# Sixteen softmax blocks per group: which engine sums which block

## The chip, the cores and the metric

The kernel runs on one core of one Trainium2 chip. The metric is the device time of one execution in microseconds (us); of several runs the median is taken. The core has five engines that run side by side, each through its own instructions in order: TensorE (PE) multiplies matrices, VectorE (DVE), ScalarE (ACT) and GpSimd (POOL) work on elements, and SyncE (SP) issues DMA transfers. GpSimd can issue transfers too[...].

## The reference

The input is `x` with 8 samples of 2048 nodes and 256 channels, and an adjacency matrix `adj` of 2048 x 2048. One layer of masked attention with 8 heads of 32 channels, a feed-forward part, and three layer normalizations:

```python
qkv = jnp.einsum('fnc,ck->fnk', x, w_qkv)
q, k, v = jnp.split(qkv, 3, axis=-1)          # each reshaped to (F, N, H, D)
scores = jnp.einsum('fnhd,fmhd->fhnm', q, k) / jnp.sqrt(D)
scores = jnp.where(adj > 0, scores, -1e9)
attn = jax.nn.softmax(scores, axis=-1)
t = jnp.einsum('fhnm,fmhd->fnhd', attn, v).reshape(F, N, C)
x1 = _layernorm(x + t, ln1_g, ln1_b)
h = jax.nn.relu(x1 @ w1 + b1)
x2 = _layernorm(x1 + h @ w2 + b2, ln2_g, ln2_b)
return layernorm(x + x2)
```

The softmax needs, for every query and head, the sum of the exponentials over all 2048 keys. This sum, the denominator, is what the change is about.

## The kernel before

**Tiling.** The queries of a sample are cut into 4 chunks of 512 (`qc`), the heads into 2 halves of 4 (`g`), the keys into 16 blocks of 128 (`mb`). An item is `(f, qc, g, mb)`; there are 1024 of them, and they are worked off in this order by one loop written out in Python, `for t, (f, qc, g, mb) in enumerate(items)`. The 16 items of one `(f, qc, g)` are called a group here; there are 64 groups.

**One item.** Two steps ahead, `scores` (L230, L233) lets TensorE multiply keys by queries for 4 heads, and VectorE adds the mask while it copies the result into an SBUF tile `p` of 128 keys x 4 heads x 512 queries (1 MiB). One step ahead, `exponentials` (L237) takes the exponential of this tile on ScalarE. In its own step, `values` (L249) multiplies the tile by the values of its keys and gathers the result over the 16 blocks in PSUM. `add_up` (L264) follows.

**The denominator.** The column sums of a group's 16 tiles are wanted. TensorE could take all 16 by a product with a matrix of ones (L315), which costs 4 matrix products each. To spare TensorE, most tiles are first added together by others:

- `POOLED`: GpSimd adds tiles into the first of them by its own additions (L271).
- `MOVED`: two chains. A DMA issued by GpSimd (L268) adds a tile to the first tile of its chain while it moves it. Each DMA of a chain has to wait until the one before it has landed, since both add into the same tile. GpSimd waits with the issue in its queue.
- `ALONE`: one tile that goes to TensorE as it is.

So four tiles are left per group, and TensorE takes the column sums of these four (`denominator`, L297), one after the other into one PSUM bank: first the one that is alone, then the first chain, the second chain, and the sum of GpSimd. The chosen blocks are before the change

```python
    POOLED = (0, 3, 6, 8, 11, 13, 15)
    MOVED = ((1, 4, 7, 10), (2, 5, 9, 12))
    ALONE = 14
```

**The order of the work around it.** The products of `scores` and `values` leave some time in each step. It is given to side jobs, which are Python generators in the list `fill`, ordered by due time: projections of the next sample, transposes, denominators, and the tails (normalization, feed-forward, output) of finished chunks. `advance(t)` resumes them at the start of a step, before `scores`, `values` and `add_up` of that step. A job that yields `MORE` goes on when there is credit, mostly one step later; one that yields `WAIT` holds its place until a given step. The denominator of a group is started two steps after the group's last block; `late` says before which step a term must not be issued (`ready` is the last block's step plus 4). In the last group, where nothing follows, blocks from 11 on (`ENDED`) go to TensorE each by itself, in an order of its own.

**What else runs on GpSimd.** In the tails it makes the small operations of a norm (`rs`, `nb`, L283 to L287), on which ScalarE waits to scale the rows (L290); four passes over a tile `y` (L459, L461, L363, L365; some 2.7 us each); and issues two loads that add `x` to `y` (L339, L367). They stand in its queue where the step that issues them puts them, ahead of that step's `add_up`.

**Tiles.** The `p` tiles come from a pool of 12. A tile is free again after its sum, its DMA or its column sum.

Of the kernel before, what the change touches and what calls it, by code (L numbers as in the profile page):

```python
# [61 lines left out]
def fast_path(ctx, tc, cst, x, adj, out, RS):  # L62
# [29 lines left out]
    def transposes(ps, src, ident=ident):  # L92
        state["credit"] -= TURN
        for j, s in enumerate(src):
            nc.tensor.transpose(ps[:, j * P:(j + 1) * P], s, ident)  # L95
# [6 lines left out]
    def bank(dt=F32):  # L102
        shape = [P, CH] if dt == F32 else [P, 2, CH]
        if state["side"] is not None:
            i = 1 - state["side"]
            return ps_x[i].tile(shape, dt, name=f"x{i}")
        i = state["turn"]
        state["turn"] = (i + 1) % 5
        pool = ps_s[i] if i < 3 else ps_x[i - 3]
        return pool.tile(shape, dt, name=f"s{i}" if i < 3 else f"x{i - 3}")  # L110
# [143 lines left out]

    POOLED = (0, 3, 6, 8, 11, 13, 15)
    MOVED = ((1, 4, 7, 10), (2, 5, 9, 12))
    ALONE = 14

    ENDED = MB - 5
    SUM = 4
# [1 line left out]
    def add_up(item):  # L264
        f, qc, g, mb = item
        for chain in MOVED:
            if mb in chain[1:] and not ((f, qc, g) == items[-1][:3] and mb >= ENDED):
                nc.gpsimd.dma_start(PT[f, qc, g, chain[0]], PT.pop(item), accum_op=ALU.add)  # L268
        if mb in POOLED[1:] and not ((f, qc, g) == items[-1][:3] and mb >= ENDED):
            first = PT[f, qc, g, POOLED[0]]  # L270
            nc.gpsimd.tensor_tensor(first, first, PT.pop(item), ALU.add)  # L271
# [24 lines left out]

    def denominator(f, qc, g, ready):  # L297
        grp = (f, qc, g)
        blocks = [ALONE] + [chain[0] for chain in MOVED + (POOLED,)]
        late = {len(blocks) - 1: ready}  # L300
        if (f, qc, g) == items[-1][:3]:
            blocks = [POOLED[0], 11, 12, MOVED[1][0], 13, 14, MOVED[0][0], 15]
            late = {n: len(items) - k for n, k in ((2, 2), (3, 1), (4, 1), (5, 0), (6, 0), (7, 0))}
        yield BANK
        ps = bank()
        for n, block in enumerate(blocks):
            if n:
                yield MORE
            while state["now"] < late.get(n, 0):
                yield WAIT  # L310
            term = PT.pop((f, qc, g, block))
            state["credit"] -= 4 * CH
            for h in range(4):
                r = D * h
                nc.tensor.matmul(ps[r:r + D, :], cst["ones"], term[:, h, :], start=(n == 0), stop=(n == len(blocks) - 1))  # L315
        dT = op.tile([P, CH], F32, name="dT")
        nc.scalar.copy(dT, ps)
        yield 1
        yield BANK
        ps = bank()  # L320
        transposes(ps, [dT[:, j::TPC] for j in range(TPC)])
        if g == 0:
            RC[f, qc] = op.tile([P, TPC, H], F32, name="rc")
        rc = RC[f, qc]
        den = ps.rearrange("p (j c) -> p j c", c=P)[:, :, ::D]
        nc.vector.reciprocal(rc[:, :, 4 * g:4 * g + 4], den)
        nc.vector.tensor_tensor(RS[:, 0], RS[:, 0], den, ALU.add)
        nc.vector.tensor_tensor(RS[:, 1], RS[:, 1], den, ALU.min)
        if g == 1:
            begin = items.index((f, qc, g, LAST)) + SUM + 2  # L330
            start(begin, outcome(f, qc) if (f, qc) != (F - 1, NCK - 1) else finish(f, qc), begin)

    def outcome(f, qc):
        yield ROOM
        state["tails"] += 1
        xin = x[f, qc * CH:(qc + 1) * CH, :].rearrange("(p j) c -> p j c", p=P)
        y = yp.tile([P, TPC, C], F32, name="y")
        yield from divide(f, qc, y)
        nc.gpsimd.dma_start(y, xin, accum_op=ALU.add)  # L339
        begin = items.index((f, qc, 1, LAST)) + SUM + 2  # L340
        if (f, qc) == (F - 1, NCK - 2):
            start(begin + 5, tail(f, qc, y, xin, 2), begin + 8)
        else:
            start(begin + 10, tail(f, qc, y, xin), begin + 26)
# [92 lines left out]
    def finish(f, qc):  # L437
        y = yp.tile([P, TPC, C], F32, name="y")
        xr, xb = state["rows"]
        yield from divide(f, qc, y)  # L440
        yT, hT = (work.tile([P, 2, CH], F32, name=n) for n in ("turned", "hT"))
        dst = out[f, qc * CH:(qc + 1) * CH, :].rearrange("(p j) c -> p j c", p=P)
        both = [half_rows(h, y, xr, xb, yT, hT, dst) for h in range(2)]
        while both:
            for e in list(both):
                if next(e, both) is both:
                    both.remove(e)
# [40 lines left out]
    def start(t, gen, due):  # L488
        fill.append([t, gen, 1, due])
        fill.sort(key=lambda e: e[3])  # L490
# [108 lines left out]
    for t, (f, qc, g, mb) in enumerate(items):  # L599
# [26 lines left out]
        if mb == LAST and t + 1 < len(items):  # L626
            start(t + 2, denominator(f, qc, g, t + SUM), t + SUM + 4)
        if t == len(items) - 3:
            start(t, denominator(f, qc, g, t), t)
# [130 lines left out]
def kernel(  # L760
# [56 lines left out]
    nc.gpsimd.memset(RS[:, 1], 1.0)  # L817

    fast_path(tc, cst, x, adj, out, RS)


# [49 lines left out]
```

## Time and profile before

| what | value |
|---|---|
| time, median of 3 runs | 3245.36 us (3242.5 to 3246.28) |
| profiled execution | 3246.02 us |
| its span, first to last instruction | 3244.1 us |
| granted TensorE clock, mean | 0.985 |
| GpSimd sums (L271) | 381, mean 4793 ns, 1825.5 us busy |
| DMAs that add (L268) | 383 of 1 MiB, median 10.4 us from issue to landing |
| masked copies on VectorE (L233) | 2048, mean 1218 ns |
| exponentials on ScalarE (L237) | 1024, mean 1910 ns |
| waits of GpSimd's queue for landed DMAs, as such (L268) | 75.5 us in 32 |
| waits of ScalarE for GpSimd's `nb` (L290) | 40.4 us in 16 |

A row of the costliest groups reads: line, engine, operation, tile written and tiles read, their shapes, the number of instructions; then the busy time in us and the mean of one in ns; then the idle time of the engine just before these instructions and what ended most of it. "PE" are the matrix products, "PEld" the loads of their stationary operand, which overlap them. In a timeline the columns are the start in us, the duration in us, then engine, line, operation and tiles, and in brackets the idle time before and its releaser. A wait for several things is put down to the one that the profile saw last.

### The profile page before, as it was taken

The numbers are of one execution on the slowest core, as the hardware profiler recorded it, in microseconds if no ns is written. First come the engines' busy times: TensorE is split into PE (matmuls) and PEld (weight loads), VectorE is DVE, ScalarE is ACT, GpSimd is POOL, SyncE is SP. The second block draws the span as 40 slices with busy tenths as digits, with TensorE's granted clock in tenths as the row PEclk, the third lists the DMA queues.
The fourth block names the chain that finished last, engine by engine and source line by source line (L and its number), as shares of the span: only waits on it lengthen the run. The fifth ranks groups of instructions, "written<-read, shape, count | busy, mean of one in ns | idle before, by whom it ended". The sixth has DMA issues, their size and how long they took to land.

```text
span 3244.1 us, 68406 instructions
## 1 busy us (share of the span) xinstructions
PE 3109.4 (96%) x28996; PEld 979.0 (30%) x28996; DVE 2735.7 (84%) x3203; ACT 2435.8 (75%) x1941; POOL 2592.2 (80%) x1358
## 2 busy tenths in 40 slices
PE   7899999999999999999999999999999999998985
PEld 4222333223332233322233323323233323332222
DVE  4888888888888888888988888888888888888975
ACT  3667778777777777778777778777778777777774
POOL 0568888888878888788887888888888788878884
PEclk8899999999999999999999999999999999999998
DMA  9688779778879788788787879878788878877763
GB/s 320 145 181 185 183 176 199 178 177 196 181 176 207 171 188 193 159 195 200 178 181 174 185 174 221 177 167 198 173 192 197 177 168 198 181 171 161 166 145 86
DMA packets 153240, 590.52 MB, mean 182 GB/s; under 512 B 15040, under 2 KB 67776, under 8 KB 103904
## 3 DMA queue, kind: packets, MB, share of 16 engines
q0 software_dynamic: 64416, 434.80, 66.9%
q1 hardware_dynamic: 87696, 149.98, 13.1%
q8 instruction: 229, 3.75, 0.4%
q10 hardware_dynamic: 816, 1.31, 0.1%
q14 instruction: 83, 0.68, 0.1%
HBM read 146.67 MB, written 37.75 MB: 57 GB/s over the span
## 4 chain that ended last, share of the span: by engine, by line
PE 75%; DVE 7%; POOL 5%; issue 4%; DMA 4%; ACT 2%; DVEq 0%; POOLq 0%; ACTq 0%
PE s L230 27%; PE x L249 24%; PE x L54 14%; PE x L315 6%; DVE p L233 6%; PE x L95 4%; DMA p<-p 3%; POOL p L271 2%; ACT p L237 1%; DMA mask<-md 1%; POOL y L365 1%; DVE st L278 1%; POOL y L363 0%; POOL y L461 0%; POOL y L459 0%
## 5 line engine op out<-in xcount | busy, mean ns | idle before, releaser
L233 DVE TENSOR_TENSOR p<-s,mask 128x1024 f32<-128x1024 f32 x2048 | 2409.3, 1218 | 372.7 <-PE s L230 209.9
L237 ACT ACTIVATE p<-p 128x2048 f32<-128x2048 f32 x1024 | 1956.1, 1910 | 521.4 <-DVE p L233 465.6
L271 POOL TENSOR_TENSOR p<-p 128x2048 f32<-128x2048 f32 x381 | 1825.5, 4793 | 223.7 <-ACT p L237 221.3
L230 PE MATMUL s<-qT,kT 32*128 32x512 f32 x8192 | 1173.8, 643 | 40.8 <-DVE p L233 35.9
L249 PE MATMUL x<-p,v 128*32 128x512 f32 x8192 | 1096.0, 607 | 16.7 <-ACT p L237 16.4
L268 POOL DMA_DIRECT2D p<-p x383 | 359.3, 956 | 306.9 <-ACT p L237 88.3
L230 PEld LDWEIGHTS s<-qT,kT 32*128 32x128 f32 x8192 | 321.1, 183 | 644.7 <-DVE p L233 587.2
L249 PEld LDWEIGHTS x<-p,v 128*32 128x32 f32 x8192 | 161.6, 108 | 797.8 <-issue 310.6
L315 PE MATMUL x<-p,ones 128*32 128x512 f32 x2080 | 268.2, 594 | 17.9 <-POOL p L271 11.1
L290 ACT ACTIVATE y<-y,nb,rs 128x256 f32<-128x256 f32 x372 | 218.7, 590 | 40.4 <-POOL nb L287 40.4
L54 PE MATMUL x<-in,wqkv 128*32 128x512 f32 x1888 | 243.5, 592 | 0.0
L278 DVE BATCH_NORM_STATS2 st<-y 128x6 f32<-128x256 f32 x372 | 154.9, 416 | 5.1 <-DMA y<-in_x_dram 5.1
L54 PE MATMUL x<-turned,w1s 128*32 128x512 f32 x992 | 123.5, 596 | 0.4 <-ACT in L166 0.4
L54 PE MATMUL x<-w2s,hT 128*32 128x256 f32 x2016 | 121.8, 382 | 2.1 <-DVE y L483 2.1
L54 PEld LDWEIGHTS x<-wqkv,in 128*32 128x32 f32 x3584 | 102.2, 110 | 63.4 <-issue 58.9
L315 PEld LDWEIGHTS x<-p,ones 128*32 128x32 f32 x2080 | 66.3, 110 | 178.2 <-issue 140.4
L54 PE MATMUL x<-wqkv,in 128*32 128x128 f32 x3584 | 117.3, 273 | 0.0
L54 PEld LDWEIGHTS x<-in,wqkv 128*32 128x32 f32 x1888 | 61.7, 110 | 140.9 <-issue 113.7
L284 POOL TENSOR_TENSOR rs<-rs,mhalf 128x4 f32<-128x4 f32 x93 | 96.3, 1036 | 7.8
L54 PEld LDWEIGHTS x<-w2s,hT 128*32 128x32 f32 x2016 | 65.4, 111 | 75.0 <-issue 33.0
L363 POOL TENSOR_TENSOR y<-y,g2r 128x1024 f32<-128x1024 f32 x31 | 82.5, 2663 | 5.3 <-ACT y L290 5.3
L461 POOL TENSOR_TENSOR y<-y,be1b2r 128x1024 f32<-128x1024 f32 x31 | 83.0, 2679 | 0.6
(116 smaller groups left out, 1335.7 us busy)
## 6 DMA issues: line engine op xcount, KB each, us to landing
p<-p POOLq DMA_DIRECT2D x383, 1024.0 KB, 10.4
in<-xd SPq DMA_DIRECT2D x87, 512.0 KB, 10.6
mask<-md SPq DMA_DIRECT2D x248, 128.0 KB, 7.9
y<-in_x_dram POOLq DMA_DIRECT2D x62, 512.0 KB, 8.1
p<-in_adj_dram SPq DMA_DIRECT2D x16, 1024.0 KB, 10.7
out_dram<-y SPq DMA_DIRECT2D x31, 512.0 KB, 6.2
in<-in_x_dram SPq DMA_DIRECT2D x29, 512.0 KB, 15.5
xd<-in SPq DMA_DIRECT2D x28, 512.0 KB, 11.2
```

Of the source, the lines that this page charges most:

```text
L54: nc.tensor.matmul(out[r:r + D], lhsT[:, r:r + D], rhs, start=start, stop=stop)
L95: nc.tensor.transpose(ps[:, j * P:(j + 1) * P], s, ident)
L230: nc.tensor.matmul(ps2[half][:, j, :], KT[f, mb // TPC, g][r:r + D, (mb % TPC) * P:(mb % TPC + 1) * P], QT[f, qc, g][r:r + D, :], start=Tr ...
L233: nc.vector.tensor_tensor(pt[:, 2 * half:2 * half + 2, :], ps, MK[f, qc, mb // 2][:, mb % 2, None, :].to_broadcast([P, 2, CH]), ALU.add)
L237: nc.scalar.activation(PT[item], PT[item], AF.Exp, scale=1.0 / math.sqrt(D))
L249: nc.tensor.matmul(O[grp][r:r + D, :], V[f, mb // TPC, g][:, mb % TPC, r:r + D], PT[item][:, h, :], start=(mb == 0), stop=(mb == LAST))
L268: nc.gpsimd.dma_start(PT[f, qc, g, chain[0]], PT.pop(item), accum_op=ALU.add)
L271: nc.gpsimd.tensor_tensor(first, first, PT.pop(item), ALU.add)
L278: nc.vector.bn_stats(st, t[:, j, :])
L284: nc.gpsimd.tensor_tensor(rs, rs, cst["mhalf"], ALU.pow)
L290: nc.scalar.activation(t[:, j, :], t[:, j, :], AF.Identity, bias=nb[:, j:j + 1], scale=rs[:, j:j + 1])
L315: nc.tensor.matmul(ps[r:r + D, :], cst["ones"], term[:, h, :], start=(n == 0), stop=(n == len(blocks) - 1))
```

## The change

Blocks 10 to 15 change hands. The DMAs take blocks 11 and 13 in place of 10 and 12; GpSimd sums 10, 12 and 14 in place of 11, 13 and 15; block 15 in place of 14 goes to TensorE as it is. TensorE reads the four tiles of a group in another order: the one alone, the first chain, GpSimd's sum, the second chain, with the sum not before `ready - 1` and the second chain not before `ready`. In the last group, where blocks from 11 on are taken singly, the two chains change places.

```diff
-    POOLED = (0, 3, 6, 8, 11, 13, 15)
-    MOVED = ((1, 4, 7, 10), (2, 5, 9, 12))
-    ALONE = 14
+    POOLED = (0, 3, 6, 8, 10, 12, 14)
+    MOVED = ((1, 4, 7, 11), (2, 5, 9, 13))
+    ALONE = 15
...
     def denominator(f, qc, g, ready):
         grp = (f, qc, g)
-        blocks = [ALONE] + [chain[0] for chain in MOVED + (POOLED,)]
-        late = {len(blocks) - 1: ready}
+        blocks = [ALONE, MOVED[0][0], POOLED[0], MOVED[1][0]]
+        late = {2: ready - 1, 3: ready}
         if (f, qc, g) == items[-1][:3]:
-            blocks = [POOLED[0], 11, 12, MOVED[1][0], 13, 14, MOVED[0][0], 15]
+            blocks = [POOLED[0], 11, 12, MOVED[0][0], 13, 14, MOVED[1][0], 15]
```

## The prediction

> **What bounds the kernel now.** I read the page first, then the waits of TensorE, then the timeline of GpSimd, TensorE and ScalarE around the waits. "Group" means the 16 blocks of one (f, qc, g); there are 64, numbered from 0. "12D" is the DMA that adds block 12 to its chain, "13P" the GpSimd sum of block 13, a "step" one block on TensorE, and the four "terms" are the four column sums of a group (L315).
>
> ```profile
> PE 3109.4 (96%) x28996; PEld 979.0 (30%) x28996; DVE 2735.7 (84%) x3203; ACT 2435.8 (75%) x1941; POOL 2592.2 (80%) x1358
> ...
> L315 PE MATMUL x<-p,ones 128*32 128x512 f32 x2080 | 268.2, 594 | 17.9 <-POOL p L271 11.1
> ```
>
> TensorE is the bound: 96% of the span, and a step with a full side job starts 2.93 us after the one before, almost without spread. So only its stalls can be won. The list of what it waited for (us, times, longest):
>
> ```profile
> PE x L249 <- ACT p L237: 16.4, 10, 5.1
> ...
> PE x L315 <- POOL p L271: 11.1, 6, 2.1
> ...
> PE x L315 <- DMA p<-p: 6.9, 5, 3.9
> ```
>
> I took the same from the start times: a term normally starts 0.88 us after the block before it, and a block's values 1.07 us after its scores. What exceeds these between 100 and 3190 us is 21.0 us ahead of terms and 21.3 us ahead of values. Both repeat once per sample (eight groups, some 388 us).
>
> **Stall A, ahead of the terms**, in group 36. GpSimd: start, us, what, idle before.
>
> ```profile
> 1861.44 1.52 POOL L268 DMA_DIRECT2D p<-p  x1
> 1863.75 0.86 POOL L268 DMA_DIRECT2D p<-p  x1 [0.80 <-ACT y L290]
> 1864.33 4.90 POOL L271 TENSOR_TENSOR p<-p 128x2048 f32<-128x2048 f32 x1
> 1875.53 0.88 POOL L268 DMA_DIRECT2D p<-p  x1 [6.30 <-ACT v L215]
> 1876.13 2.67 POOL L363 TENSOR_TENSOR y<-y,g2r 128x1024 f32<-128x1024 f32 x1
> 1878.45 4.89 POOL L271 TENSOR_TENSOR p<-p 128x2048 f32<-128x2048 f32 x1
> 1883.01 2.65 POOL L365 TENSOR_TENSOR y<-y,be2r 128x1024 f32<-128x1024 f32 x1
> 1885.96 0.89 POOL L367 DMA_DIRECT2D y<-in_x_dram  x1 [0.30 <-POOL y L365]
> 1886.57 4.84 POOL L271 TENSOR_TENSOR p<-p 128x2048 f32<-128x2048 f32 x1
> ```
>
> These are 9D, 10D, 11P, 12D, L363, 13P, L365, L367, 15P. 12D must follow 9D of its own chain, which lands at 1875.0 in the trace. So it stands 6.3 us at the head of an in-order queue, and 13P and 15P, whose blocks have been ready for long, stand behind it. (The releaser printed there, a ScalarE copy, is not what it waited for; the landing is.) Then 12D lands at 1886.2 and 15P ends at 1891.4, and TensorE stops for both:
>
> ```profile
> 1886.22 1.06 PE L315 MATMUL x<-p,ones 128*32 128x512 f32 x8 [1.33 <-DMA p<-p]
> ...
> 1891.46 1.06 PE L315 MATMUL x<-p,ones 128*32 128x512 f32 x8 [2.11 <-POOL p L271]
> ```
>
> **Stall B, ahead of the values**, in group 27. Here 10D waits for 7D, and 11P and a norm's four small operations follow:
>
> ```profile
> 1427.29 0.86 POOL L268 DMA_DIRECT2D p<-p  x1 [7.21 <-issue]
> 1427.85 4.88 POOL L271 TENSOR_TENSOR p<-p 128x2048 f32<-128x2048 f32 x1
> ```
>
> The norm's result `nb` is out at 1434.7, and ScalarE, in order, has the next exponentials behind the row scaling that needs it:
>
> ```profile
> 1434.73 0.60 ACT L290 ACTIVATE y<-y,nb,rs 128x256 f32<-128x256 f32 x1 [4.05 <-POOL nb L287]
> ```
>
> TensorE loses 2.26 us there.
>
> **The change, part by part.** *Work.* Six sums and six DMAs per group stay; in the last group one DMA becomes one sum. TensorE's order, its term places and the orders of DVE, ACT and SP stay as they are; GpSimd's order alone changes, with which block each term reads. So there is no work to save, and all lies in the waits.
>
> *Blocks 10 to 13 swap kinds* (10P, 11D, 12P, 13D). In group 36, with the same durations (sum 4.6 us start to start, issue 0.6, L363 and L365 2.4): block 10's exponential ends 1860.1, so 10P runs 1863.0 to 1867.6; 11D issues at once (7D landed 1863.2); 12P 1868.2 to 1872.8; L363 to 1875.2; 13D meets the landing of 9D at about 1875.5, 0.3 us instead of 6.3; L365 to 1878.5; 14P to 1883.1. The sum is read by the third term, due 1884.7 without stalls: 1.6 us of room. 13D is given 12D's 10.65 us and lands at 1886.2; the fourth term is due at 1887.7: 1.5 us of room. The stall of 3.80 goes. The fifth groups of samples (12, 20, 28, 36, 44, 52) stalled 2.51 + 2.26 + 1.79 + 3.80 + 1.79 + 3.56 = 15.7 us; by the same reckoning the room left for 13D is 2.6, 2.9, 2.8, 1.5, 3.1 and 1.6 us, so all go. Group 30 gives 0.4. Group 1 lost 4.87 to 12D; the fourth term is due at 194.2 and 13D hardly lands before 12D's 195.4, so 1.2 stays and 3.7 go. A: 19.8 us.
>
> *The same swap at B.* In group 27 10P fits into the idle time (block 10 ready 1419.4: 1420.0 to 1424.6); 11D takes over the wait for 7D (landed 1426.8) at 1427.3, but no sum stands between it and the norm: `nb` comes at about 1430, when ScalarE gets there only at 1430.7. The fourth groups (11, 19, 27, 35, 43, 51, 59) lost 1.42 + 1.69 + 2.26 + 1.91 + 0.90 + 1.97 + 5.13 = 15.3; in group 59 the norm comes out about 4.9 us earlier against a 5.1 us stall, so 0.3 stays. B: 15.0. Group 31's 1.2 us comes behind 8P, which does not move: kept.
>
> *The clock.* The granted clock falls beside some stalls (columns: PE, PEld, DVE, ACT, POOL busy, clock, DMA share, GB/s):
>
> ```profile
> 1112.00:1116.00 4.00, 4.00 (x22) 0.86 (x19) 1.88 (x2) 2.88 (x3) 3.83 (x4) 0.57 0.05 13
> ```
>
> That follows the 2.2 us stall of group 20 and adds 0.83 + 0.82 us. The Trainium skill ("TensorE: Matmul & The Clock Gate", Part 1) has the clock fall only after an idle window of about 3.4 us. By the rule only the 5.1 us stall of group 59 could cost more than itself (0.82 + 0.58); by the row three stalls do (1.65, 1.70 in group 51, 1.40): 4.75. I take the row.
>
> *Terms.* Block 15 as the term read alone needs its exponential, which TensorE's own values already waited for: nothing. The sum moves from fourth to third term, its last addend from 15 to 14: equal in steps. The second chain moves one term later with its last block one later: equal too. Here a rule would make it easy: the skill ("DMA: Bandwidth & Descriptors", Anatomy of one DMA) gives a GpSimd DMA 2.0 us plus bytes over 436 per ns; for 1 MiB an estimate of 4.4 us, leaving 13D some 7.7 us of room in group 36. The rows say median 10.4 to landing, 6.8 to 17.5. By the rule A could not exist, since 9D would have landed at 1866; the row decides, and the room is 1.5.
>
> *Cost not seen in the trace*: 13D landing later than 12D did. From below 0; from above, each microsecond costs up to 6 us in the six tight groups once 1.5 to 3 us are used. Late landings of 2 us in half of them give a few microseconds; I take 5, range 0 to 20.
>
> *Last group.* 10P ends about 3188, its term starts 3191.3; the chain 1, 4, 7 is read early, 2, 5, 9 late. Nothing.
>
> **Sum** against the profiled execution (3246.0 us, span 3244.1; the runs' median is 3245.4): 3246.0 - 19.8 - 15.0 - 4.75 + 5 = 3211.5. With all stalls and their clock losses gone (21.0 + 21.3 + 6.6) it would be 3197.
>
> **Rivals.** *Half of it* (0.18): B stays, because another GpSimd operation, such as 12P or L459, takes the place of 11P ahead of the norm; or A does not go. Then 3246 - 19.8 - 1.7 = about 3224. For it: GpSimd is 80% busy. Against: in group 27 the 7.2 us idle is long enough for the whole 10P. *No gain* (0.07): the waits reappear one step later, or the stalls only hide slack elsewhere: 3246. Against: VectorE is at 84% and steps are as long as TensorE's own work.
>
> *The second chain becomes what is late* (0.10, slower). Four sums now stand two steps apart (8, 10, 12, 14) with at most 5.9 us per pair, against 4.6 plus an issue; tail passes of 2.4 us and norms of 1.9 fall between, and 13D stands behind 12P. If it came 7 us later, the fourth term would wait 4.6 us in the six fifth groups (room 2.4 on average), 3.5 in the six third (3.5) and 2.8 in the six seventh (4.2): 65 us, A not won: 3246 - 15.0 - 4.75 + 65 = 3291. It decides from 18d - 60.6 = 39.5, d = 5.6 us. Against: where the room is short, 12D is held by the landing of 9D and not by GpSimd, and 10P and 12P fill just that idle time.
>
> **The numbers.** The main case has 0.65 and its own range 3200 to 3222; with half of it the range is 3200 to 3234. A difference of 0.2% (6.5 us) is about what a measurement of this kernel can tell from none. Faster 0.85 (main, half, a little of the third), same 0.05, slower 0.10.
>
> **What would show it.** Right: GpSimd no longer idle 6 to 7 us ahead of the last DMA of a chain; the term waits on the sum near zero; fewer waits of ScalarE for `nb`; TensorE's share at 97%. Wrong: waits of the terms for DMA growing above 20 us, or `nb` waits unchanged.

## The result and the profile after

The changed kernel takes 3198.33 us (median of 4 runs, 3195.77 to 3199.43) against 3243.93 us before (4 runs, 3240.75 to 3246.28): a ratio of 0.9859, 95% interval 0.9842 to 0.9876. It is 1.4% faster, 45.6 us by the medians. 3211.5 us was forecast, in a range from 3200 to 3234: the direction and the mechanism are right, the gain is a third larger than forecast, and the time lies 1.7 us below the range. The forecast started from one profiled execution, 3246.0 us, which is 2.1 us above the median of the four; against that median the same savings would have given 3209.4 us.

The span of the profiled execution fell from 3244.1 to 3197.5 us. The page after, the lines that answer to those of before, and the row of the scaling that ScalarE does in a norm:

```profile
PE 3098.8 (97%) x28996; PEld 980.3 (31%) x28996; DVE 2737.4 (86%) x3203; ACT 2438.4 (76%) x1941; POOL 2589.4 (81%) x1358
...
L315 PE MATMUL x<-p,ones 128*32 128x512 f32 x2080 | 267.1, 592 | 0.6 <-DMA p<-p 0.5
...
L290 ACT ACTIVATE y<-y,nb,rs 128x256 f32<-128x256 f32 x372 | 218.4, 590 | 3.0 <-POOL nb L287 3.0
```

Before, the row of the scaling was

```profile
L290 ACT ACTIVATE y<-y,nb,rs 128x256 f32<-128x256 f32 x372 | 218.7, 590 | 40.4 <-POOL nb L287 40.4
```

The counts of TensorE, VectorE and ScalarE are those of before, and GpSimd's busy time moved by 3 us. No engine has less to do. What fell is the idle time at the ends of the two rows: 17.9 to 0.6 us ahead of the terms, 40.4 to 3.0 us ahead of the scaling. In the list of TensorE's waits:

```profile
PE x L315 <- DMA p<-p: 0.5, 1, 0.5
...
PE x L249 <- ACT p L237: 0.2, 1, 0.2
```

The line "PE x L315 <- POOL p L271" is no longer in it. Taken from the start times, between 100 and 3190 us: what the pieces of TensorE's work start later than their normal spacing (the median for each pair of neighbours; from 0.1 us counted) fell from some 67 to some 21 us, by 46, about the change of the span (46.6). The largest wait in TensorE's list, that of the scores (L230) for VectorE, is hardly touched: 35.9 us before, 35.6 after.

Group 36 after, on GpSimd:

```profile
1837.81 1.51 POOL L268 DMA_DIRECT2D p<-p  x1
1838.38 5.54 POOL L271 TENSOR_TENSOR p<-p 128x2048 f32<-128x2048 f32 x1
1842.90 1.87 POOL L268 DMA_DIRECT2D p<-p  x1
1844.02 5.37 POOL L271 TENSOR_TENSOR p<-p 128x2048 f32<-128x2048 f32 x1
1848.55 3.17 POOL L363 TENSOR_TENSOR y<-y,g2r 128x1024 f32<-128x1024 f32 x1
1851.92 0.88 POOL L268 DMA_DIRECT2D p<-p  x1 [0.20 <-issue]
1852.53 2.66 POOL L365 TENSOR_TENSOR y<-y,be2r 128x1024 f32<-128x1024 f32 x1
1854.85 4.88 POOL L271 TENSOR_TENSOR p<-p 128x2048 f32<-128x2048 f32 x1
```

This is 9D, 10P, 11D, 12P, L363, 13D, L365, 14P, with no hole of 6 us. 9D takes as long to land as before (13.6 us, at 1851.4) and 13D as long as 12D did (10.6 us, at 1862.6). But when 13D comes to the head of the queue, 9D has just landed: 0.20 us of idle time in place of 6.30. The sum ends at 1859.7 and its term is issued at 1861.1; the fourth term is issued at 1864.0. The room for 13D is 1.4 us; 1.5 was forecast.

Group 27 after, GpSimd first:

```profile
1411.83 0.87 POOL L268 DMA_DIRECT2D p<-p  x1 [2.06 <-issue]
...
1414.45 0.19 POOL L287 TENSOR_SCALAR nb<-nb 128x4 f32<-128x4 f32 x1
```

and ScalarE, which no longer waits for `nb` (no brackets, so no idle time):

```profile
1415.79 0.59 ACT L290 ACTIVATE y<-y,nb,rs 128x256 f32<-128x256 f32 x1
```

11D still waits for the landing of 7D, but 10P now fills most of the time: 2.06 us of idle time are left of 7.21, and the norm follows 11D directly.

### The profile page after: what moved, and what is told of

Same layout as the page of the kernel before. It is cut to its first block, busy times and chain, and to the rows that moved or that the text cites. A ratio compares the mean times of both kernels' runs of the same rounds, so it can differ in the third digit from the quotient of the medians.

```text
span 3197.5 us, 68542 instructions
## 1 busy us (share of the span) xinstructions
PE 3098.8 (97%) x28996; PEld 980.3 (31%) x28996; DVE 2737.4 (86%) x3203; ACT 2438.4 (76%) x1941; POOL 2589.4 (81%) x1358
## 4 chain that ended last, share of the span: by engine, by line
PE 87%; DVE 5%; issue 2%; DMA 1%; POOL 1%; ACT 1%; DVEq 0%; ACTq 0%; POOLq 0%
PE s L230 32%; PE x L249 28%; PE x L54 16%; PE x L315 7%; DVE p L233 4%; PE x L95 4%; DMA p<-p 1%; DVE st L278 0%; POOL p L271 0%; DMA y<-in_x_dram 0%; DVE y L353 0%; ACT p L237 0%; PE s L54 0%; DVE mv L279 0%; ACT y L290 0%
## 5 line engine op out<-in xcount | busy, mean ns | idle before, releaser
L271 POOL TENSOR_TENSOR p<-p 128x2048 f32<-128x2048 f32 x382 | 1858.7, 4866 | 388.5 <-ACT p L237 388.2
L230 PE MATMUL s<-qT,kT 32*128 32x512 f32 x8192 | 1172.4, 642 | 40.9 <-DVE p L233 35.6
L230 PEld LDWEIGHTS s<-qT,kT 32*128 32x128 f32 x8192 | 320.8, 183 | 643.9 <-DVE p L233 602.5
L268 POOL DMA_DIRECT2D p<-p x382 | 408.1, 1070 | 78.4 <-ACT p L237 49.4
L315 PE MATMUL x<-p,ones 128*32 128x512 f32 x2080 | 267.1, 592 | 0.6 <-DMA p<-p 0.5
L315 PEld LDWEIGHTS x<-p,ones 128*32 128x32 f32 x2080 | 67.4, 110 | 156.8 <-issue 152.0
L363 POOL TENSOR_TENSOR y<-y,g2r 128x1024 f32<-128x1024 f32 x31 | 99.3, 3205 | 1.9 <-ACT y L290 1.9
L365 POOL TENSOR_TENSOR y<-y,be2r 128x1024 f32<-128x1024 f32 x31 | 91.9, 2963 | 0.6
```

Source lines behind the costliest of these rows:

```text
L230: nc.tensor.matmul(ps2[half][:, j, :], KT[f, mb // TPC, g][r:r + D, (mb % TPC) * P:(mb % TPC + 1) * P], QT[f, qc, g][r:r + D, :], start=Tr ...
L363: nc.gpsimd.tensor_tensor(z, z, rows(cst["g2r"]), ALU.mult)
```

## The experiments

Two theories were held against each other first. **Queue theory**: a DMA that waits for its chain stands at the head of GpSimd's queue, and what is late is what stands behind it. **Order theory**: what helps is only that the second chain gets a step more before TensorE reads it. Four kernels take the change apart; each was timed beside the kernel before on the same chip.

**Terms only.** The terms' order of the change over the blocks of before:

```diff
-        blocks = [ALONE] + [chain[0] for chain in MOVED + (POOLED,)]
-        late = {len(blocks) - 1: ready}
+        blocks = [ALONE, MOVED[0][0], POOLED[0], MOVED[1][0]]
+        late = {2: ready - 1, 3: ready}
```

> The blocks of before, with only the order of the terms changed (sum third, second chain fourth). Queue theory (a transfer waiting at the head of GpSimd's queue holds up the sums and norms behind it): the queue is as before, so the sum's last addition ends as late as before but is read one step (2.93 us) earlier; the fifth groups wait some 33 us in all where they waited 15.7, the norms' stalls stay at some 21 us; about 3262 us, slower than before. Order theory (what helps is that the second chain gets one step more): the term waits go, about 3224 us.

Measured: 3262.2 us, ratio 1.0064 (1.0044 to 1.0084). The third term waits 33.2 us in all, 32.8 of it in the fifth groups. In TensorE's timeline of the group that was shown:

```profile
1899.76 1.94 PE L315 MATMUL x<-p,ones 128*32 128x512 f32 x8 [6.36 <-POOL p L271]
```

The queue is as before, and the sum is asked for a step (2.9 us) sooner. So the order of the terms is no gain by itself; order theory falls.

**Blocks only.** The blocks of the change, terms as before (the diff above, reversed, on the changed kernel).

> The blocks of the change, with the order of the terms of before (second chain third, sum last). Queue theory: the stalls behind norms are gone (0 to 4 us left), waits of terms on the sum are gone, but the chain that ends with block 13 is read 2.93 us earlier than in the change and lands too late in some 12 groups by 0.3 to 3.6 us, 16 us in all; about 3214 us (3208 to 3220). Order theory: the blocks alone bring nothing, about 3244 us.

Measured: 3219.4 us, ratio 0.9934 (0.9915 to 0.9953). Only one wait of ScalarE for `nb` is left (3.0 us), no term waits for the sum by more than 0.3 us, and the third term, now the second chain's, waits 19.5 us: 4.0 in the second groups of samples, 7.0 in the third, 8.1 in the fifth. 16 was expected. The blocks alone bring 24 us and the terms alone lose 19; together they bring 46. Each part removes a wait that the other would meet.

**One half of the swap: 10 and 11.**

```diff
-    POOLED = (0, 3, 6, 8, 11, 13, 15)
-    MOVED = ((1, 4, 7, 10), (2, 5, 9, 12))
+    POOLED = (0, 3, 6, 8, 10, 13, 15)
+    MOVED = ((1, 4, 7, 11), (2, 5, 9, 12))
```

In the last group the two chains change places, as in the change.

> Only blocks 10 and 11 change hands (chain 1, 4, 7, 11; sums 3, 6, 8, 10, 13, 15; block 14 alone; terms as before). Queue theory, with two stalls apart: the stall behind norms in the fourth groups goes (15 to 18 us, and 2 to 3 us of low clock), the stall ahead of terms in the fifth groups stays near 21 us; about 3224 us (3218 to 3230). If both stalls have one cause, 3200 us; if this is not the cause of the norms' lateness, 3244 us.

Measured: 3229.2 us, ratio 0.9961 (0.9945 to 0.9977), at the upper end of what was expected. The waits of the values for ScalarE fell from 16.4 to 1.7 us in TensorE's list; those of the terms did not:

```profile
PE x L315 <- DMA p<-p: 12.9, 12, 3.5
PE x L315 <- POOL p L271: 10.0, 6, 2.1
```

The wait for the sum is nearly as before (11.1). The wait for transfers has grown from 6.9: 12D now follows one step behind 11D, and in the third groups, where the second chain cost nothing, it now comes 7.1 us too late in all (in group 18 12D took 17.1 us to land in place of 14.6). So the two stalls can be parted: 11D waiting with no sum behind it leaves the norms on time, while 12D still holds the sum.

**The other half: 12 and 13.**

```diff
-    POOLED = (0, 3, 6, 8, 11, 13, 15)
-    MOVED = ((1, 4, 7, 10), (2, 5, 9, 12))
+    POOLED = (0, 3, 6, 8, 11, 12, 15)
+    MOVED = ((1, 4, 7, 10), (2, 5, 9, 13))
```

> Only blocks 12 and 13 change hands (chain 2, 5, 9, 13; sums 3, 6, 8, 11, 12, 15; block 14 alone; terms as before). Queue theory, with two stalls apart: waits of terms on the sum go (some 12 us), waits of terms on the second chain stay (some 9 us, or a few more, since its last transfer is no earlier), the stalls behind norms stay near 21 us; about 3231 us (3225 to 3240). If both stalls have one cause, 3200 us.

Measured: 3240.1 us, ratio 0.9994 (0.9984 to 1.0004), a hair above the expected range, and not to be told from no change. The fourth term's waits fell from 12.9 to 0.7 us as expected; the third term's rose from 8.1 to 18.0, since block 13 comes a step after block 12 and is read in the old place. Two things were not expected. The waits of the values for ScalarE, which should have stayed, fell from 16.4 to 9.9 us, though 10D waits in the queue about as long as before (6.8 us in group 27, 7.2 before); why they fell is not shown, and the profiled execution (3235.5 us) is the fastest of the ten. And a wait grew that had no place in the forecast. Timeline of all engines:

```profile
2308.43 2.67 POOL L461 TENSOR_TENSOR y<-y,be1b2r 128x1024 f32<-128x1024 f32 x1
...
2311.13 0.69 DVE L483 TENSOR_TENSOR y<-x,y 128x512 f32<-128x512 f32 x1 [4.10 <-POOL y L461]
...
2311.88 2.58 PE L54 MATMUL x<-w2s,hT 128*32 128x256 f32 x32 [2.56 <-DVE y L483]
```

The pass L461 over `y` is one more piece of work in GpSimd's queue. VectorE waits for it before it can take the feed-forward's result out of PSUM, and TensorE waits for that bank. With sums 11 and 12 next to each other, TensorE came 8.1 us late at this place in all. In the kernel before the same chain is there:

```profile
1538.83 0.69 DVE L483 TENSOR_TENSOR y<-x,y 128x512 f32<-128x512 f32 x1 [2.13 <-POOL y L461]
...
1539.57 1.93 PE L54 MATMUL x<-w2s,hT 128*32 128x256 f32 x32 [0.93 <-DVE y L483]
```

It is a third stall behind GpSimd's queue: 2.8 us in four places, or 3.6 with two other short waits of the feed-forward, one of them for ScalarE. In the changed kernel TensorE has none of it.

**Queue order alone.** If the place in the queue counts, the blocks need not change at all. Each block stays with the engine that had it; the last DMA of a chain is issued behind the next sum (10D behind 11P, 12D behind 13P), with the terms' order of the change:

```diff
         for chain in MOVED:
             if mb in chain[1:] and not ((f, qc, g) == items[-1][:3] and mb >= ENDED):
-                nc.gpsimd.dma_start(PT[f, qc, g, chain[0]], PT.pop(item), accum_op=ALU.add)
+                if mb == chain[-1] and (f, qc, g) != items[-1][:3]:
+                    state["held"] = chain[0], mb
+                else:
+                    nc.gpsimd.dma_start(PT[f, qc, g, chain[0]], PT.pop(item), accum_op=ALU.add)
...
             nc.gpsimd.tensor_tensor(first, first, PT.pop(item), ALU.add)
+            if state.get("held"):
+                head, block = state.pop("held")
+                nc.gpsimd.dma_start(PT[f, qc, g, head], PT.pop((f, qc, g, block)), accum_op=ALU.add)
```

> The blocks of before, each summed by the engine that summed it before; only the last transfer of each chain (blocks 10 and 12) is issued behind the next GpSimd sum (11 and 13), and the terms are read in the order of the change. Queue theory: it is the place in the queue that counts, not which block; the stalls behind norms and ahead of terms go nearly as far as in the change, about 3205 us (3199 to 3214). Spacing theory (the change helps because its transfers stand further apart and so land sooner, median 9.7 in place of 10.4 us): transfers 9 and 10 are still close together, so no gain or a loss, 3240 us or more.

Measured: 3199.7 us, ratio 0.9858 (0.9842 to 0.9875): the whole gain, and the terms' new order alone (the first run here) had been a loss. GpSimd in group 36 (lines are shifted; L271 and L277 are the DMAs, L274 the sum):

```profile
1838.51 1.52 POOL L271 DMA_DIRECT2D p<-p  x1
1840.27 4.58 POOL L274 TENSOR_TENSOR p<-p 128x2048 f32<-128x2048 f32 x1 [0.24 <-ACT p L237]
1844.80 0.87 POOL L277 DMA_DIRECT2D p<-p  x1
1845.41 2.67 POOL L369 TENSOR_TENSOR y<-y,g2r 128x1024 f32<-128x1024 f32 x1
1847.73 4.87 POOL L274 TENSOR_TENSOR p<-p 128x2048 f32<-128x2048 f32 x1
1852.24 1.19 POOL L277 DMA_DIRECT2D p<-p  x1
```

9D, 11P, 10D, L369, 13P, 12D: the landing of 9D, here at 1851.9, is waited for behind finished work. The term waits are 1.6 us in all. As a test against the spacing theory the run is weaker than its expectation says: holding a DMA behind a sum also moves 9D and 10D apart (6.3 us in place of 2.3). What speaks against spacing are the traces: the landings that the queue waits for come no sooner. 9D in the six fifth groups took 12.4 us on average before the change and 12.7 after it, 7D in the seven fourth groups 12.5 and 12.4. Only the last transfer of the second chain came a little sooner in the fifth groups, 10.5 in place of 10.9 us, against stalls of 1.8 to 3.8. A kernel with the transfers spread and GpSimd still blocked was not run.

**How close the second chain is.** In the changed kernel blocks 13 and 14 change hands, so that the chain ends later:

```diff
-    POOLED = (0, 3, 6, 8, 10, 12, 14)
-    MOVED = ((1, 4, 7, 11), (2, 5, 9, 13))
+    POOLED = (0, 3, 6, 8, 10, 12, 13)
+    MOVED = ((1, 4, 7, 11), (2, 5, 9, 14))
```

> The change with blocks 13 and 14 exchanged (chain 2, 5, 9, 14; sums 3, 6, 8, 10, 12, 13): the last transfer comes a step and a sum later. It measures the room of the second chain. If the room is what the trace of the change shows (1.4 to 2.9 us in the fifth groups, 1.7 us in the third), a transfer issued some 4.9 us later in the third groups makes the fourth term wait about 3 us in six or seven of them, 15 to 25 us in all: about 3218 us. If the room is ample, 3198 us.

Measured: 3273.1 us, ratio 1.0082 (1.0064 to 1.0099), 75 us over the changed kernel. The row of the terms:

```profile
L315 PE MATMUL x<-p,ones 128*32 128x512 f32 x2080 | 273.9, 605 | 50.2 <-DMA p<-p 50.2
```

The direction is right, size and place are not: the fourth term waits 29.7 us in the fifth groups, 15.3 in the seventh, 5.0 in the first and 0.1 in the third, which were expected to pay. In group 36 14D is issued at 1895.2, behind 13P and L365; 9D had landed at 1887.0. The fourth term then stands:

```profile
1904.85 1.07 PE L315 MATMUL x<-p,ones 128*32 128x512 f32 x8 [3.12 <-DMA p<-p]
```

Some 20 us more are lost at the steps next to these waits, where the clock is low in eleven places between 200 and 3000 us. So the slower rival of the forecast is real, one block further than the change goes.

**The one large stall that is left.** Near its end the changed kernel stops once, as the kernel before did (6.5 us there). Timeline of all engines:

```profile
3081.76 0.43 DVE L278 BATCH_NORM_STATS2 st<-y 128x6 f32<-128x256 f32 x1 [5.23 <-DMA y<-in_x_dram]
...
3084.20 2.09 PE L230 MATMUL s<-qT,kT 32*128 32x512 f32 x8 [6.61 <-DVE p L233]
```

VectorE waits there for the rows of x of the last chunk but one. Its tail was started later:

```diff
-            start(begin + 5, tail(f, qc, y, xin, 2), begin + 8)
+            start(begin + 7, tail(f, qc, y, xin, 2), begin + 8)
```

> The change, with the tail of the last chunk but one started two steps later (begin + 7 in place of begin + 5). In the trace of the change TensorE stops once for 6.3 us near the end, with VectorE waiting 5.1 us for the rows of x that this tail normalizes, and low clock behind it. If that wait is all: 6 to 8 us less, about 3191 us. If the chunk's own end then becomes what ends the kernel: 3198 us or more.

Measured: 3195.7 us, ratio 0.9849 (0.9833 to 0.9866). The stall shrank to 1.6 us, but one of 3.0 us came behind it, and the idle stretch in the last chunk's end grew from 5.2 to 7.6. With one step in place of two (begin + 6), beside the changed kernel run again:

> The change, with the tail of the last chunk but one started one step later (begin + 6). In the run with two steps the stall of 6.6 us near the end shrank, but one of 3.0 us came behind it and the last idle stretch grew from 5.2 to 7.6 us. If the two trade against each other step by step, one step gives about what two did, 3195.5 us; if one step is enough for the rows of x to land without delaying the end, 3192 us.

> The changed kernel as it is, on the same chip beside the version above: 3198 us.

Measured: 3196.5 us (0.9856, 0.9838 to 0.9873) and 3197.7 us (0.9861, 0.9841 to 0.9881). Neither version can be told from the change. With two steps the stall was traded for others.

## Why the prediction came out too small

By its own steps, with what the traces measured:

| step | forecast, us | measured, us |
|---|---|---|
| A, waits of terms that go | 19.8 | 20.0 (20.9 to 0.9), with 0.75 of low clock in group 1 |
| B, waits of values behind a norm that go | 15.0 | 16.5 |
| low clock beside stalls that go | 4.75 | 6.6 |
| new waits, block 13 landing late | -5 | nothing beside the 0.9 left in A |
| waits of the feed-forward | not in the sum | 3.6, of it 2.8 for L461 |
| sum | 34.5 | 46.7 |

B is the seven fourth groups (15.3) and group 31 (1.2); low clock is the three stalls counted (4.75) and group 1 (1.85); the sum stands beside the 46 us by which all lateness fell.

**The step that failed** is the term "late landings of 2 us in half of them give a few microseconds; I take 5, range 0 to 20". In its place the trace after shows no wait for a late 13D in the six fifth groups. The rooms left for 13D, forecast as 2.6, 2.9, 2.8, 1.5, 3.1 and 1.6 us, measured 0.3, 2.9, 2.9, 1.5, 2.7 and 2.2. One landing was late: in group 12 9D took 15.0 us in place of 12.3, so 13D ate 2.3 us of its room and cost nothing, and the sum behind it made the third term wait 0.25 us. The rest of the 0.9 us is 0.7 in group 1, where 1.2 had been counted as staying. Nor did the 5 follow from the forecast's own rooms: with landings 2 us late in all six groups, only 36 and 52 would have waited, 0.5 and 0.4 us.

**What was missed** is the third piece of work in GpSimd's queue, L461, which the forecast put at nothing. The list of waits of the kernel before had it:

```profile
DVE y L483 <- POOL y L461: 9.5, 6, 2.1
...
PE x L54 <- DVE y L483: 2.1, 4, 0.9
```

The forecast followed the queue to the sums and to `nb` and stopped there. Smaller terms: group 31 was expected to keep 1.2 us and kept none, group 59 lost its 0.3 too, and the low clock of group 1 (1.85, and 0.75 that stands under A as if it were a wait for 12D) was not counted.

**The range** ended at 3200 although the text put the case of all stalls gone at 3197 (3199 without 1.8 us of low clock that stand in it twice). The stalls that the forecast followed went nearly whole, and the range should have reached their sum. The 1.7 us by which the result lies below it are less than the 2.1 us between the execution that served as base and the median; by how little the range missed is chance.

What was right: that no work is saved, and only GpSimd's order changes; which groups stall, and what for; that the swap at 10 and 11 cures the norms and the one at 12 and 13 the sum, shown by the two halves (though the second also took 6.5 us from the waits behind norms); that the second chain needs its later place, shown by the blocks alone; that the low clock goes with the stalls. The rule of 2.0 us plus bytes (the Trainium skill, "DMA: Bandwidth & Descriptors", Anatomy of one DMA), by which stall A could not have been, is not what these transfers follow: by an estimate from it 1 MiB takes 4.4 us, and it took a median of 10.4 us to land before the change and 9.7 after.

Of the rivals, "half of it" did not come. The slower one came in the run with block 14: in group 36 14D was issued 8.3 us after the landing of 9D, where 12D and 13D were issued 0.5 us after it; 7.7 us later is past the rival's point of 5.6. (That point counts A as won; with A not won, as in the rival's own 3291 us, its rooms give 4.5.) Of the three kinds of groups that it named, the fifth and seventh paid about what it said, and the third paid nothing.

## What to carry to other kernels

An instruction that must wait belongs behind the ready work of its queue, not ahead of it: with the same sums and the same transfers, moving two DMAs per group behind a sum, with the readers' order suited to it, was worth 1.4%. When such a wait is found, follow everything that stands behind it to the engine that sets the end; here it was the sums, the norms and a pass over `y`, and each had its own way to TensorE. When a schedule is loosened in one place, check the readers: the new blocks brought half the gain with the old order of reading, and the new order of reading alone lost.

## What the runs showed of the hardware

The granted clock of TensorE fell after shorter idle times than the rule weighed in the forecast has it. The rule (the Trainium skill, "TensorE: Matmul & The Clock Gate", Part 1) asks for some 3.4 us. After matmul gaps of 1.9 to 2.1 us (2.0 at 1109 us in the kernel before; 1.9, 2.1 and 1.9 in the run with blocks 10 and 11) a stretch of 3.4 us at half clock followed; after gaps of 2.0, 2.2 and 2.1 us in the kernel before (721, 1435 and 1889 us) none did. Over all eleven traces, between 200 and 3000 us: none of the gaps under 1.9 us was followed by low clock, 9 of the 19 gaps from 1.9 to 2.6 us were, and all 15 longer ones, up to 6.4 us, had it. What decides between the 19 is not shown. The changed kernel has no gap of 1.9 us there and no low clock. So a stall of 2 us cost up to 1.7 us more than itself (1.65 and 1.70 in the kernel before), but not each time.
